# A first layer merged by a list scheduler: new weights, a longer lag, ranks for ties, and one affine folded into the MLP

## The chip, the cores and the metric

The kernel runs on one core of one Trainium2 chip. It computes two layers of a small vision network on 8 images of 64 x 64 pixels with 192 channels, all in float32. The metric is the device time of one execution in microseconds; before the change the median of three runs is 25196.08 us (25184.54 to 25197.58).

The core has five engines with a queue each, served in order: TensorE (PE: products and transposes; PEld is its weight load), VectorE (DVE), ScalarE (ACT: activations, from function tables that must be loaded), GpSimd (POOL), and SyncE (SP), which issues the transfers (DMA). An engine stalls when the head of its queue waits for another engine. So the order in which independent work is placed in the queues decides how long the engines stand idle.

## The reference

Each layer is `x = x + layer(groupnorm(x))`. Layer 0 is a block of two 3x3 depthwise convolutions, a state-space mixer and an MLP; layer 1 is a selective scan in four directions. The change is in layer 0, which is, cut to what matters:

```python
c1 = dwconv2d(x, cpe1_w, cpe1_b)                     # 3x3, per channel
xs = x + c1
h = layernorm(xs, ln1_w, ln1_b)                      # first norm
zxbcdt = h @ in_proj_w.T                             # z: 384, xBC: 512, dt: 6 columns
dt = softplus(dt + dt_bias)
xBC = silu(causal_conv1d(xBC, conv1d_w, conv1d_b))   # 4 taps
y = ssd(xm, dt, A, Bm, Cm, chunk)                    # chunked state-space mixer
y = (y + xm * D_skip) * silu(z)
y = y * rsqrt(mean(y * y) + 1e-05) * rms_w
x2 = xs + y @ out_proj_w.T
x2 = x2 + dwconv2d(x2, cpe2_w, cpe2_b)
h2 = layernorm(x2, ln2_w, ln2_b)                     # second norm: (x2 - mean) * rstd * w + b
m = gelu(h2 @ fc1_w.T + fc1_b) @ fc2_w.T + fc2_b
return x2 + m
```

## The kernel before

Layer 0 works on 64 tiles of 512 pixels (8 images of 8 tiles). Its work is written as 18 chains (Python generators), one for each stage, and each chain goes through all tiles. A chain yields steps: an engine, a weight (the time in us that the author expects of it), and the instructions. `Flow` merges the chains into one order for each engine, before anything runs, by a clock of its own: it always takes the step that can start first.

```python
class Flow:
    LAG, TABLE, STAY, RANK = 0.25, 1.3, 0.0, 0.01

    def chain(self, gen, rank=None, ready=0.0):
        self.chains.append([gen, next(gen), ready, len(self.chains) if rank is None else rank])

    def start(self, req, ready):
        # ... "wait" for another chain's mark, "take" of a buffer: come at once when possible
        engine, _, _, after, table = req
        t = max(ready if after is None else after, self.free[engine])
        if engine == "ACT" and table and table != self.table:
            return t + self.TABLE + self.STAY, t + self.TABLE
        return t, t

    def run(self):
        while self.chains:
            best = None
            for i, (_, req, ready, rank) in enumerate(self.chains):
                s = self.start(req, ready)
                if s and (best is None or s[0] + self.RANK * rank < best[0]):
                    best = s[0] + self.RANK * rank, s[1], i
            # ...
                engine, weight, do, _, table = req
                # ... the instructions are recorded, kept in this order on their engine
                t += weight
                self.free[engine] = t
                t += self.LAG          # from then on a dependent step may start
```

Layer 0 sets `f.RANK = -0.01`, so that with equal starts the chain that was entered later goes first; they are entered from the back of the network (MLP) to its front (statistics). The numbers of buffers are set there too and stay as they are:

```python
        f = Flow(tc)
        f.RANK = -0.01
        for tag, n in (("mm", 5), ("sm", 3), ("xin", 2), ("xs", 3), ("h", 3), ("cin", 2), ("cv", 2), ("zs", 2),
                       ("dt", 2), ("e", 5), ("yt", 4), ("yc", 1), ("xx", 3), ("x2", 1), ("m", 1), ("sq", 1), ("s2", 1), ("ld", 3), ("csr", 1), ("xdt", 1), ("xw", 1), ("t1", 1)):
            f.pool(tag, n)
```

`mm` and `sm` are PSUM banks, for wide and for small products. The stages that the text speaks of:

```python
        def conv(out, src, w, b):                # both 3x3 convolutions; line 325 is the tap
            for ct in range(CT):                 # CT = 2 halves of 96 channels
                r[ct] = yield step("ACT", 0.75, ...)      # first tap: scale and bias
            for j in range(1, 9):
                for ct in range(CT):
                    r[ct] = yield step("DVE", 0.75, lambda: [nc.vector.scalar_tensor_tensor(...)], r[ct])

        def norm(xs, w, b, key):
            # GpSimd adds the halves, PE takes the mean (ln_m), DVE subtracts, ACT squares,
            # GpSimd adds, PE takes the variance (ln_v), ACT: rs = exp(-0.5 * ln(var + eps))
            yield step("DVE", 1.25, lambda: [nc.vector.tensor_mul(h, h, bc(rs, 1, [CP, CT, TT]))])
            for ct in range(CT):                 # line 386: the affine
                r = yield step("ACT", 0.8, lambda: [
                    nc.scalar.activation(h[:, ct], h[:, ct], AF.Identity, bias=b[:, ct : ct + 1], scale=w[:, ct : ct + 1])])

        def rows_of(T, da):                      # running sums of the decays, for the e tiles
            # PE p_cs (line 598), ACT copies it to csr, SP writes csr to DRAM (csd)
        def decays():                            # SP reads csd back, spread over 128 rows, as e[T, c], 4 a tile
        def powers():
            # ACT: six Relu with a bias for each head (line 634), then one Exp (line 639), on e
        def scores():
            # PE p_g (line 654), DVE gm = p_g * mask, DVE e = e * gm (line 663)
        def turn():
            # PE p_t (transposes), DVE xdt and xw from it (lines 686, 691); PE p_b, ACT bt
        def states():
            # PE p_i, DVE t1; PE p_n, DVE st (the running state)
        def mixer():
            # PE p_y: three products with dsk (line 768), six with e and xdt (line 771);
            # DVE yt = t1 + p_y, yt = yt * zs
        def output():
            # ACT yt * rq, PE p_u (transposes), ACT yc, PE p_o, DVE xx = p_o + xs
        def mlp():
            # PE p_f (line 937, weights wf1 on h), ACT gelu (line 913, bias fb1), PE p_f (line 957), DVE, SP stores
```

At the end the chains are entered and merged:

```python
        for gen in (mlp, norm2, conv2, output, mixer, states, turn, scores, powers, decays, steps_in_time, convolve, mix, gate, norm1, conv1, inputs, statistics):
            f.chain(gen())
        f.run()
```

Layer 1 is drawn up by the same class with its standard figures in its short front and end parts, and by a fixed loop in its scan.

Of the kernel before, what the change touches and what calls it, by code (L numbers as in the profile page):

```python
# [16 lines left out]
CP, CT = 96, 2  # L17
# [168 lines left out]
def layer0(tc, consts, x, x1s, mv1, w_in, w_out, w_fc1, w_fc2, rows):  # L186
# [12 lines left out]
    with ExitStack() as ctx:  # L199
# [17 lines left out]
        nc.sync.dma_start(out=wf1, in_=w_fc1.rearrange("(t p) m -> p t m", p=CP))  # L217
        wf2 = wp.tile([128, 6, C], F32, name="wf2")
        nc.sync.dma_start(out=wf2, in_=w_fc2.rearrange("(t p) m -> p t m", p=128))
        rv = wp.tile([128, 12], F32, name="rv")  # L220
        nc.sync.dma_start(out=rv, in_=rows.partition_broadcast(128))
        dtb, an = rv[:, 0:6], rv[:, 6:12]
# [12 lines left out]
            nc.gpsimd.memset(t, 0.0)  # L235

        f = Flow(tc)
        f.RANK = -0.01
        for tag, n in (("mm", 5), ("sm", 3), ("xin", 2), ("xs", 3), ("h", 3), ("cin", 2), ("cv", 2), ("zs", 2),
                       ("dt", 2), ("e", 5), ("yt", 4), ("yc", 1), ("xx", 3), ("x2", 1), ("m", 1), ("sq", 1), ("s2", 1), ("ld", 3), ("csr", 1), ("xdt", 1), ("xw", 1), ("t1", 1)):  # L240
            f.pool(tag, n)
# [28 lines left out]
        def inputs():  # L270
            for T, (b, t) in enumerate(tiles):
                yield "wait", ("gn", b)
                yield "take", "xin"
                xin = got["xin", T] = xins[T % 2]
                lo, hi = max(0, t * RT - 1), min(HI, t * RT + RT + 1)
                at = lo - (t * RT - 1)

                def load():
                    out = []
                    for edge, row in ((t == 0, 0), (t == NT - 1, RT + 1)):  # L280
                        if edge:
                            f.keep(nc.gpsimd.memset(xin[:, :, row : row + 1, :], 0.0))
                    for ct in range(CT):
                        out.append(
                            nc.sync.dma_start(
                                out=xin[:, ct, at : at + hi - lo, 1 : WI + 1], in_=im(image(b)[:, ct, lo * WI : hi * WI])
                            )
                        )
                    return out

                r = yield step("SP", 0.2, load)
                sc, sh = got["gn", b]
                for ct in range(CT):
                    v = xin[:, ct, at : at + hi - lo, 1 : WI + 1]
                    r = yield step(
                        "ACT",
                        0.85,
                        lambda: [
                            nc.scalar.activation(v, v, AF.Identity, bias=sh[:, ct : ct + 1], scale=sc[:, ct : ct + 1])
                        ],  # L300
                        r + 4 if ct == 0 else None,
                    )
                f.at["in", T] = r

        def conv(out, src, w, b):

            tap = lambda ct, j: src[:, ct, j // 3 : j // 3 + RT, j % 3 : j % 3 + WI]
            r = [0.0] * CT
            for ct in range(CT):
                r[ct] = yield step(  # L310
                    "ACT",
                    0.75,
                    lambda: [
                        nc.scalar.activation(  # L314
                            im(out[:, ct]), tap(ct, 0), AF.Identity, bias=b[:, ct : ct + 1], scale=w[:, ct, 0:1]
                        )
                    ],
                )
            for j in range(1, 9):
                for ct in range(CT):  # L320
                    r[ct] = yield step(
                        "DVE",
                        0.75,
                        lambda: [
                            nc.vector.scalar_tensor_tensor(  # L325
                                im(out[:, ct]), tap(ct, j), w[:, ct, j : j + 1], im(out[:, ct]), ALU.mult, ALU.add
                            )
                        ],
                        r[ct],
                    )  # L330
            return max(r)
# [7 lines left out]
                f.give("xin", r)  # L339
                f.at["conv1", T] = r  # L340

        def norm(xs, w, b, key):

            yield "take", "h"
            h = got[key] = lnp.tile([CP, CT, TT], F32, name="h", bufs=3)
            both = lambda src: [nc.gpsimd.tensor_add(s2, src[:, 0], src[:, 1])]  # L346
            mean = lambda ps: [nc.tensor.matmul(ps[:CP], ones96, s2, start=True, stop=True)]
            yield "take", "s2"
            s2 = lnp.tile([CP, TT], F32, name="s2")
            yield step("POOL", 1.25, lambda: both(xs))  # L350
            yield "take", "mm"
            pm = mp.tile([128, TT], F32, name="ln_m", tag="mm")
            r = yield step("PE", 0.95, lambda: mean(pm))
            f.give("s2", r)
            r = yield step("DVE", 1.25, lambda: [nc.vector.tensor_sub(h, xs, bc(pm[:CP], 1, [CP, CT, TT]))])
            f.give("mm", r)
            yield "take", "sq"
            sq = lnp.tile([CP, CT, TT], F32, name="sq")
            yield step("ACT", 1.06, lambda: [nc.scalar.activation(sq, h, AF.Square)])  # L359
            yield "take", "s2"  # L360
            s2 = lnp.tile([CP, TT], F32, name="s2")
            r = yield step("POOL", 1.25, lambda: both(sq))
            f.give("sq", r)
            yield "take", "mm"
            pv = mp.tile([128, TT], F32, name="ln_v", tag="mm")
            r = yield step("PE", 0.95, lambda: mean(pv))
            f.give("s2", r)
            rs = lnp.tile([CP, TT], F32, name="rs", bufs=2)
            r = yield step(
                "ACT",  # L370
                1.3,
                lambda: [
                    nc.scalar.activation(rs, pv[:CP], AF.Ln, bias=eps[:CP]),
                    nc.scalar.activation(rs, rs, AF.Exp, scale=-0.5),
                ],
                None,
                "explog",
            )
            f.give("mm", r)
            yield step("DVE", 1.25, lambda: [nc.vector.tensor_mul(h, h, bc(rs, 1, [CP, CT, TT]))])  # L380
            for ct in range(CT):
                r = yield step(
                    "ACT",
                    0.8,
                    lambda: [
                        nc.scalar.activation(
                            h[:, ct], h[:, ct], AF.Identity, bias=b[:, ct : ct + 1], scale=w[:, ct : ct + 1]
                        )
                    ],
                )  # L390
            return r

        def norm1():
            for T in range(len(tiles)):
                yield "wait", ("conv1", T)
                f.at["h1", T] = yield from norm(got["xs", T], v96["l1w"], v96["l1b"], ("h1", T))

        def h1_done(T, r):
            if last := f.part(("h1", T), 2, r):
# [44 lines left out]
        def convolve():  # L444

            for T, (b, t) in enumerate(tiles):
# [9 lines left out]
                for pair in ((0, 1), (2, 3)):  # L456
                    for mt in pair:
                        yield "wait", ("cin", T, mt)
                        done[mt] = yield step(
                            "ACT",  # L460
                            0.68,
                            lambda: [
                                nc.scalar.activation(
                                    dst[mt],
# [7 lines left out]
                    for k in range(1, 4):  # L472
                        for mt in pair:
                            done[mt] = yield step(
                                "DVE",
                                0.9,
                                lambda: [
                                    nc.vector.scalar_tensor_tensor(
                                        dst[mt],
# [144 lines left out]
        def powers():  # L624

            for T in range(len(tiles)):
                for c in range(NQ):
# [1 line left out]
                    e, cs = got["e", T, c], got["cst", T]  # L629
                    yield step(  # L630
                        "ACT",
                        1.8,
                        lambda: [
                            nc.scalar.activation(e[:, h], e[:, h], AF.Relu, bias=cs[:, c, h : h + 1], scale=-1.0)
                            for h in range(NH)
# [6 lines left out]
        def scores():  # L642

            for T in range(len(tiles)):
                yield "wait", ("cv", T)
                bm, cm = got["bm", T], got["cm", T]
                for c in range(NQ):
# [12 lines left out]
                    yield "wait", ("p", T, c)  # L660
                    e = got["e", T, c]
                    f.at["e", T, c] = yield step(
                        "DVE", 0.95, lambda: [nc.vector.tensor_mul(e, e, bc(gm, 1, [128, NH, Q]))]
                    )

        def turn():
# [38 lines left out]
        def states():  # L705

            st = None
            for T, (b, t) in enumerate(tiles):
# [5 lines left out]
                for c in range(NQ):  # L714
# [23 lines left out]
                    else:  # L738
                        yield step(
                            "DVE",  # L740
                            0.55,
                            lambda: [nc.vector.tensor_mul(hv(new), hv(st), bc(dec[:NS, 2, c], 2, [NS, NH, HD]))],
                            0.0,
                        )
# [5 lines left out]
        def mixer():  # L750

            for T, (b, t) in enumerate(tiles):
# [3 lines left out]
                for c in range(NQ):  # L756
# [24 lines left out]
                    if t or c:  # L781
# [2 lines left out]
                        q = yield step("DVE", 0.55, lambda: [nc.vector.tensor_add(yt, t1, py)])  # L784
                        f.give("sm", q)
                        f.give("t1", q)
                        q = yield step("DVE", 0.62, lambda: [nc.vector.tensor_mul(yt, yt, zs[:, c])])
                    else:
                        q = yield step("DVE", 0.55, lambda: [nc.vector.tensor_mul(yt, py, zs[:, c])])
                        f.give("sm", q)  # L790
# [13 lines left out]
        def output():  # L804

            for T, (b, t) in enumerate(tiles):
# [14 lines left out]
                yc = tp.tile([128, 3, TT], F32, name="yc")  # L821
                for c in range(NQ):
                    yt = got.pop(("yt", T, c))
                    q = yield step("ACT", 0.52, lambda: [nc.scalar.activation(yt, yt, AF.Copy, scale=rs[:, c : c + 1])], r)
                    yield "take", "sm"
                    pt = qp.tile([128, DIN], F32, name="p_u", tag="sm")
                    q = yield step(
# [69 lines left out]
        def norm2():  # L897
            for T, (b, t) in enumerate(tiles):
# [2 lines left out]
                yield "take", "ld"  # L901
                xr = got["xr", T] = ld.tile([CP, CT, TT], F32, name="xr", tag="ld")
                yield step("SP", 0.1, lambda: [nc.sync.dma_start(out=xr, in_=image(b)[:, :, t * TT : t * TT + TT])])
                f.at["h2", T] = yield from norm(x2, v96["l2w"], v96["l2b"], ("h2", T))
                r = yield step("POOL", 2.7, lambda: [nc.gpsimd.tensor_add(xr, xr, x2)])
                f.give("x2", r)
                f.at["xr", T] = r
# [1 line left out]
        def keep_mlp(T, mt, m, ps, p):  # L909
            r = yield step(  # L910
                "ACT",
                0.69,
                lambda: [nc.scalar.activation(m[:, mt], ps, AF.Gelu, bias=v128["fb1"][:, mt : mt + 1])],  # L913
                p,
                "gelu",
            )
# [70 lines left out]
                if t == NT - 1:  # L987
                    yield step("DVE", 0.5, lambda: aggregate(nc, mv1[:, b], stats1))

        for gen in (mlp, norm2, conv2, output, mixer, states, turn, scores, powers, decays, steps_in_time, convolve, mix, gate, norm1, conv1, inputs, statistics):  # L990
            f.chain(gen())
        f.run()


# [825 lines left out]
```

## Time and profile before

| what | value |
|---|---|
| time, median of 3 | 25196.08 us |
| span of the profiled run | 25211.5 us |
| TensorE busy | 21347.4 us (85%) |
| VectorE busy | 21583.5 us (86%) |
| ScalarE busy | 21653.2 us (86%) |
| GpSimd busy | 16862.8 us (67%) |
| layer 0, from the timeline | 0 to about 5675 us |
| layer 1, the rest | about 19537 us |

The shares are means over two layers with different limits, so layer 0 has to be read from its own stretch. A stretch line gives the busy time of each engine in it, the number of instructions in brackets, and then the clock that TensorE was granted as a part of full speed. In a group's line, the first number after the bar is the busy time, the second the mean of one instruction in ns, and behind the next bar stands the idle time of the engine just before such instructions, with what ended it. The chain of waits is followed back from the last instruction: at each step to what released it.

### The profile page before, as it was taken

Reading aid. Unit: us, or ns where it says so; the run is one execution under the profiler, and the core shown is the slowest. Engines: PE = TensorE matmul, PEld = TensorE weight load, DVE = VectorE, ACT = ScalarE, POOL = GpSimd, SP = SyncE. Lnnn points to the kernel's source line nnn. Section 1 sums busy time; section 2 is a strip of 40 time slices with the busy share of each in tenths; the row PEclk is TensorE's granted clock in tenths of the full one; section 3 lists DMA queues with packets and bytes.
Section 4 is the critical chain, followed back from the end, with each engine's and each line's share of the span. In section 5 each row is a group of like instructions: output and inputs, shape, how many; then the busy total and the mean of one; then the engine's idle time right before and its main releaser. Section 6 shows DMA issues by size and latency. Waiting matters only on the chain.

```text
span 25211.5 us, 312991 instructions
## 1 busy us (share of the span) xinstructions
PE 21347.4 (85%) x100012; PEld 10381.6 (41%) x100012; DVE 21583.5 (86%) x22090; ACT 21653.2 (86%) x38251; POOL 16862.8 (67%) x13639
## 2 busy tenths in 40 slices
PE   7888888887888888888888888888888888888888
PEld 3444444443443444344434443444344434443444
DVE  6777667658999899899989998999899989988998
ACT  5666566558998999899989998999899989998998
POOL 0111111116997799599959995999599959986997
PEclk7888888888999999999999999999999999999999
DMA  1111111112222222222222222222222222222222
GB/s 45 38 36 42 37 37 42 33 28 88 66 66 76 78 65 69 85 68 65 66 88 66 66 66 87 66 66 69 85 67 67 64 89 65 67 66 87 66 66 59
DMA packets 1129703, 1608.06 MB, mean 64 GB/s; under 512 B 259360, under 2 KB 458432, under 8 KB 1118848
## 3 DMA queue, kind: packets, MB, share of 16 engines
q1 hardware_dynamic: 1128064, 1588.03, 22.4%
q8 instruction: 806, 13.21, 0.2%
q14 instruction: 833, 6.82, 0.1%
HBM read 1024.65 MB, written 160.17 MB: 47 GB/s over the span
## 4 chain that ended last, share of the span: by engine, by line
POOL 55%; PE 23%; issue 9%; DVE 6%; ACT 4%; DMA 3%; SPq 1%; POOLq 0%; DVEq 0%; ACTq 0%
POOL hc L1575 49%; POOL cy L1573 4%; DVE xs L1165 3%; PE p_f L937 2%; PE y L1590 2%; PE p_x L429 2%; PE p_f L957 2%; PE p_z L512 2%; POOL du L1454 1%; DMA xc<-xo 1%; PE p_y L771 1%; DVE xs L325 1%; PE p_o L854 1%; PE p_o L1339 1%; PE p_y L768 1%
## 5 line engine op out<-in xcount | busy, mean ns | idle before, releaser
L1575 POOL TENSOR_TENSOR hc<-hs,cb 128x1024 f32<-128x1024 f32 x6144 | 14582.9, 2374 | 10.4 <-POOL cy L1573 6.1
L1561 DVE TENSOR_TENSOR_SCAN hs<-ea,cy,g 128x512 f32<-128x512 f32 x10752 | 13058.6, 1263 | 787.6 <-PE g L1545 425.4
L1519 ACT ACTIVATE pw<-duT,bt 128x384 f32<-128x384 f32 x16384 | 8873.2, 601 | 12.8 <-DVE duT L1467 12.8
L1590 PE MATMUL y<-hc,sel 128*64 128x512 f32 x24576 | 6655.0, 620 | 2467.4 <-POOL hc L1575 2461.7
L1534 ACT ACTIVATE ea<-dr,an 128x512 f32<-128x512 f32 x12288 | 8125.5, 709 | 348.9 <-DVE hs L1561 326.2
L1545 PEld LDWEIGHTS g<-ident,pw 128*128 128x128 f32 x49152 | 5306.8, 141 | 4303.0 <-issue 2670.4
L1545 PE MATMUL g<-ident,pw 128*128 128x128 f32 x49152 | 6773.8, 280 | 30.6 <-DVE hs L1561 12.9
L1590 PEld LDWEIGHTS y<-hc,sel 128*64 128x64 f32 x24576 | 1228.9, 135 | 3886.9 <-POOL hc L1575 3627.0
L1573 POOL COPY cy<-hs 128x2 f32<-128x2 f32 x6144 | 1165.1, 190 | 1547.2 <-DVE hs L1561 1482.2
L1454 POOL TENSOR_TENSOR du<-de,xc 128x512 f32<-128x512 f32 x768 | 983.4, 1280 | 1639.2 <-DVE de L1447 1621.1
L1561 DVE TENSOR_TENSOR_SCAN hs<-ea,g 128x512 f32<-128x512 f32 x1536 | 1776.9, 1204 | 178.1 <-PE g L1545 122.7
L346 POOL TENSOR_TENSOR s<-x 96x512 f32<-96x512 f32 x64 | 88.5, 1383 | 2366.9 <-DVE x L325 2169.7
L346 POOL TENSOR_TENSOR s<-sq 96x512 f32<-96x512 f32 x128 | 221.2, 1728 | 1049.2 <-ACT sq L359 909.8
L1433 PE MATMUL p_dt<-xdbl,wd 13*128 13x512 f32 x1536 | 857.3, 639 | 41.4 <-DVE de L1447 39.5
L1165 DVE SCALAR_TENSOR_TENSOR xs<-pad,p,xs 128x4096 f32<-128x4096 f32 x192 | 860.8, 4484 | 36.9 <-ACT xs L1155 29.7
L1404 PE MATMUL p_d<-xc,wx 128*44 128x512 f32 x1536 | 792.1, 598 | 96.3 <-DMA xc<-xo 96.3
L937 PE MATMUL p_f<-h,wf 96*128 96x512 f32 x1536 | 786.4, 656 | 4.8 <-ACT m L913 3.3
L325 DVE SCALAR_TENSOR_TENSOR x<-xx,p,x 96x512 f32<-96x512 f32 x1024 | 720.2, 744 | 29.3 <-ACT x L314 29.1
L1447 DVE SCALAR_TENSOR_TENSOR de<-p_dt,spa 128x512 f32<-128x512 f32 x768 | 524.0, 682 | 255.6 <-ACT spa L1442 253.4
L325 DVE SCALAR_TENSOR_TENSOR xs<-xin,p,xs 96x512 f32<-96x512 f32 x1024 | 702.0, 755 | 17.2 <-ACT xs L314 17.2
L957 PE MATMUL p_f<-m,wf 128*96 128x512 f32 x1536 | 711.3, 614 | 0.8 <-ACT m L913 0.8
L1601 DVE TENSOR_TENSOR yacc<-yacc,y 128x512 f32<-128x512 f32 x576 | 624.6, 1084 | 18.5 <-PE y L1590 18.5
(199 smaller groups left out, 20330.1 us busy)
## 6 DMA issues: line engine op xcount, KB each, us to landing
cb<-cd SPq DMA_DIRECT2D x4096, 128.0 KB
dr<-de SPq DMA_DIRECT2D x3072, 128.0 KB
xc<-xo SPq DMA_DIRECT2D x256, 768.0 KB
e<-csd SPq DMA_DIRECT2D x256, 384.0 KB
xl<-x SPq DMA_DIRECT2D x256, 384.0 KB
xo<-xs SPq DMA_DIRECT2D x48, 1024.0 KB
xo<-xt SPq DMA_DIRECT2D x24, 2048.0 KB
xl<-in_x SPq DMA_DIRECT2D x64, 384.0 KB
```

The lines of the kernel that those rows point to most:

```text
L325: nc.vector.scalar_tensor_tensor(im(out[:, ct]), tap(ct, j), w[:, ct, j : j + 1], im(out[:, ct]), ALU.mult, ALU.add)
L937: nc.tensor.matmul(ps, wf1[:, ct, mt * 128 : mt * 128 + 128], h[:, ct], start=ct == 0, stop=ct == 1)
L957: nc.tensor.matmul(ps[:CP], wf2[:, kt, ct * CP : ct * CP + CP], m[:, kt], start=kt == 0, stop=kt == 5)
L1165: nc.vector.scalar_tensor_tensor(xs, tap(j), kw[:, d, j : j + 1], xs, ALU.mult, ALU.add)
L1454: o(nc.gpsimd.tensor_mul(st["du", d], st["de", d], st["xc"][:, d]))
L1519: nc.scalar.activation(st["pw", p, j][:, :, i], st["duT"][:, j].rearrange("p (g c) -> p g c", c=64), AF.Copy, scale=st["bt"][:, j, n : n + 1],
L1534: nc.scalar.activation(ea[:, f], state[s]["dr", d][:, f], AF.Exp, scale=an[:, k, p, at : at + 1])
L1545: nc.tensor.transpose(g[:, f, j * 128 : j * 128 + 128], state[s]["pw", p, j][:, 2 * d + f].rearrange("p a b -> p (a b)"), ident,)
L1561: nc.vector.tensor_tensor_scan(rev(h[:, f]), rev(ea[:, f]), rev(g[:, f]), 0.0 if first(s) else state[s - 1]["cy"][:, p, d, f : f + 1], ALU ...
L1573: o(nc.gpsimd.tensor_copy(st["cy"][:, p, d], h[:, :, last]))
L1575: o(nc.gpsimd.tensor_mul(hc, h, bc(st["cb", p], 1, [128, 2, TT])))
L1590: o(nc.tensor.matmul(y[half[f]], sel, hc[:, f], start=p == 0 and k > 0, stop=p == NP1 - 1))
```

## The change

The change draws the merged order of layer 0 anew and removes one small piece of its work.

- The weights of steps are set to what a profile measured, the lag after a step goes from 0.25 to 0.684 us, a switch of ScalarE's function table counts 0.464 us less in the choice of the next step (though not on the scheduler's clock), and each chain gets a rank of its own, which now decides ties only.
- The second norm's scale and shift (`ln2_w`, `ln2_b`) are applied to the first MLP product once, at the start: `wf1` is multiplied by the scale, and `fb1` becomes `fc1_b + fc1_w @ ln2_b`. The norm then ends with the multiplication by `rs`. The first norm keeps its affine.

```diff
+        ps = mp.tile([128, TT], F32, name="p_fb", tag="mm")
+        for mt in range(6):
+            for ct in range(CT):
+                nc.tensor.matmul(
+                    ps[:, mt : mt + 1],
+                    wf1[:, ct, mt * 128 : mt * 128 + 128],
+                    v96["l2b"][:, ct : ct + 1],
+                    start=ct == 0,
+                    stop=ct == 1,
+                )
+        fb1 = wp.tile([128, 6], F32, name="fb1")
+        nc.vector.tensor_add(fb1, ps[:, 0:6], v128["fb1"])
+        for ct in range(CT):
+            nc.vector.tensor_scalar_mul(wf1[:, ct], wf1[:, ct], v96["l2w"][:, ct : ct + 1])
 ...
-        f.RANK = -0.01
+        f.LAG, f.STAY, f.RANK = 0.684, -0.464, -0.01
 ...     # weights (engine, before -> after)
         # inputs' affine ACT 0.85 -> 0.92, first tap of conv ACT 0.75 -> 0.81
-        def norm(xs, w, b, key):
+        def norm(xs, key, w=None, b=None):
-            yield step("POOL", 1.25, lambda: both(xs))        # and both(sq)
+            yield step("POOL", 1.6, lambda: both(xs))
-            yield step("DVE", 1.25, lambda: [nc.vector.tensor_mul(h, h, bc(rs, 1, [CP, CT, TT]))])
-            for ct in range(CT):
+            r = yield step("DVE", 1.4, lambda: [nc.vector.tensor_mul(h, h, bc(rs, 1, [CP, CT, TT]))])
+            for ct in range(CT if w is not None else 0):
 ...     # causal convolution: first tap ACT 0.68 -> 0.81, further taps DVE 0.9 -> 0.77
         # powers: six Relu ACT 1.8 -> 2.35; scores: e * gm DVE 0.95 -> 1.02
         # states: st * dec DVE 0.55 -> 0.6; mixer: yt * zs DVE 0.62 -> 0.66; output: yt * rq ACT 0.52 -> 0.62
-                f.at["h2", T] = yield from norm(x2, v96["l2w"], v96["l2b"], ("h2", T))
+                f.at["h2", T] = yield from norm(x2, ("h2", T))
-                lambda: [nc.scalar.activation(m[:, mt], ps, AF.Gelu, bias=v128["fb1"][:, mt : mt + 1])],
+                lambda: [nc.scalar.activation(m[:, mt], ps, AF.Gelu, bias=fb1[:, mt : mt + 1])],
 ...
-        for gen in (mlp, norm2, conv2, output, mixer, states, turn, scores, powers, decays, steps_in_time, convolve, mix, gate, norm1, conv1, inputs, statistics):
-            f.chain(gen())
+        for gen, rank in (
+            (mlp, -0.177), (norm2, -0.056), (conv2, -0.275), (output, -0.03), (mixer, -0.08), (states, -0.04),
+            (turn, -0.06), (scores, 0.017), (powers, -0.284), (decays, -0.195), (steps_in_time, 0.209),
+            (convolve, 0.071), (mix, -0.12), (gate, -0.17), (norm1, -0.14), (conv1, -0.254),
+            (inputs, -0.313), (statistics, -0.298),
+        ):
+            f.chain(gen(), rank)
         f.run()
```

More of the change, by code (lines that the diff above doesn't have):

```diff
@@ L296, in inputs @@
                         "ACT",
-                        0.85,
+                        0.92,
                         lambda: [
@@ L311, in conv @@
                     "ACT",
-                    0.75,
+                    0.81,
                     lambda: [
@@ L361, in norm @@
             s2 = lnp.tile([CP, TT], F32, name="s2")
-            r = yield step("POOL", 1.25, lambda: both(sq))
+            r = yield step("POOL", 1.6, lambda: both(sq))
             f.give("sq", r)
@@ L395, in norm1 @@
                 yield "wait", ("conv1", T)
-                f.at["h1", T] = yield from norm(got["xs", T], v96["l1w"], v96["l1b"], ("h1", T))
+                f.at["h1", T] = yield from norm(got["xs", T], ("h1", T), v96["l1w"], v96["l1b"])
         def h1_done(T, r):
@@ L460, in convolve @@
                             "ACT",
-                            0.68,
+                            0.81,
                             lambda: [
@@ L475, in convolve @@
                                 "DVE",
-                                0.9,
+                                0.77,
                                 lambda: [
@@ L631, in powers @@
                         "ACT",
-                        1.8,
+                        2.35,
                         lambda: [
@@ L662, in scores @@
                     f.at["e", T, c] = yield step(
-                        "DVE", 0.95, lambda: [nc.vector.tensor_mul(e, e, bc(gm, 1, [128, NH, Q]))]
+                        "DVE", 1.02, lambda: [nc.vector.tensor_mul(e, e, bc(gm, 1, [128, NH, Q]))]
                     )
@@ L740, in states @@
                             "DVE",
-                            0.55,
+                            0.6,
                             lambda: [nc.vector.tensor_mul(hv(new), hv(st), bc(dec[:NS, 2, c], 2, [NS, NH, HD]))],
@@ L786, in mixer @@
                         f.give("t1", q)
-                        q = yield step("DVE", 0.62, lambda: [nc.vector.tensor_mul(yt, yt, zs[:, c])])
+                        q = yield step("DVE", 0.66, lambda: [nc.vector.tensor_mul(yt, yt, zs[:, c])])
                     else:
@@ L823, in output @@
                     yt = got.pop(("yt", T, c))
-                    q = yield step("ACT", 0.52, lambda: [nc.scalar.activation(yt, yt, AF.Copy, scale=rs[:, c : c + 1])], r)
+                    q = yield step("ACT", 0.62, lambda: [nc.scalar.activation(yt, yt, AF.Copy, scale=rs[:, c : c + 1])], r)
                     yield "take", "sm"
@@ L988, in mlp @@
                     yield step("DVE", 0.5, lambda: aggregate(nc, mv1[:, b], stats1))
-        for gen in (mlp, norm2, conv2, output, mixer, states, turn, scores, powers, decays, steps_in_time, convolve, mix, gate, norm1, conv1, inputs, statistics):
-            f.chain(gen())
+        for gen, rank in (
+            (mlp, -0.177),
+            (norm2, -0.056),
+            (conv2, -0.275),
+            (output, -0.03),
+            (mixer, -0.08),
+            (states, -0.04),
+            (turn, -0.06),
+            (scores, 0.017),
+            (powers, -0.284),
+            (decays, -0.195),
+            (steps_in_time, 0.209),
+            (convolve, 0.071),
+            (mix, -0.12),
+            (gate, -0.17),
+            (norm1, -0.14),
+            (conv1, -0.254),
+            (inputs, -0.313),
+            (statistics, -0.298),
+        ):
+            f.chain(gen(), rank)
         f.run()
```

## The prediction

> **What bounds the kernel now.** I read the page's span and slices first, then the busy time in stretches, then the chain of waits and the groups of layer 0. The slices show two programs: slices 1 to 9 with GpSimd almost idle (layer 0), the rest with GpSimd near full (layer 1). The timeline puts the last product of layer 0 at 5674 us, so layer 0 is 5675 us, 88.3 us for each of its 64 tiles (with 25 us of start taken off). Layer 1 is the other 19537 us, and the diff touches nothing in it.
>
> ```profile
> span 25211.5 us, 312991 instructions
> ...
> DVE  6777667658999899899989998999899989988998
> ACT  5666566558998999899989998999899989998998
> POOL 0111111116997799599959995999599959986997
> PEclk7888888888999999999999999999999999999999
> ```
>
> The stretch 600 to 5600 us is layer 0 in its steady state; two stretches of 90 us inside it are a bad and a good one (columns: length; busy time and instructions of PE, PEld, DVE, ACT and POOL in this order; granted TensorE clock, DMA share, GB/s).
>
> ```profile
> 600.00:5600.00 5000.00, 4375.39 (x13789) 2174.94 (x13789) 3480.66 (x5788) 3049.40 (x5662) 603.20 (x481) 0.85 0.14 37
> ```
>
> ```profile
> 2670.00:2760.00 90.00, 67.68 (x212) 34.75 (x212) 47.87 (x81) 33.79 (x68) 2.87 (x4) 0.74 0.10 23
> ```
>
> ```profile
> 2220.00:2310.00 90.00, 87.88 (x288) 41.50 (x287) 75.77 (x123) 66.38 (x114) 13.03 (x9) 1.00 0.17 45
> ```
>
> No engine is full. TensorE's 88% is time at a granted clock of 0.85. With full-clock durations (0.857 us for a 512-column product, 2.16 us for the nine of one y, and so on) the products of a tile add up to 60.3 us. VectorE is busy 70% of 88.3, or 61.5 us a tile, ScalarE 61%, or 53.9 us. So the floor of a tile is near 62 us, and 26 us are lost to waits in the merged order. The mean is 248 TensorE instructions in 90 us; the good stretch did 288, a tile in 88.3 x 248/288 = 76 us, with the clock at 1.00. The bad one did 212, a tile in 103 us.
>
> Why it is bad shows in the chain of waits there (start, length, what).
>
> ```profile
> 2652.25 0.98 PE p_cs L598 x8
> 2653.26 0.57 ACT csr L603
> 2653.86 1.51 DMA csd<-csr
> 2655.43 5.37 DMA e<-csd
> 2660.82 1.87 ACT e L634 x6
> ...
> 2698.02 1.30 PE p_y L771 x12
> 2699.34 5.54 DMA e<-csd
> 2704.95 1.87 ACT e L634 x6
> 2706.85 0.85 ACT e L639
> 2707.72 0.96 DVE e L663
> ...
> 2719.11 10.61 DVE xs L325 x16
> 2729.71 0.48 DVE xw L691
> 2730.24 0.27 PE p_b L696
> ```
>
> Two things to see: the decay tile e comes too late (product, copy, two transfers, seven activations, 14 us with nothing else on the chain), and sixteen taps of the first convolution stand as one block of 10.6 us on VectorE, with a 0.48 us operation behind them that TensorE wants.
>
> I added the whole chain over 600 to 5600 us by engine: PE 3475, DVE 605, ACT 516, DMA 167, POOL 82, issue 62 us. At 56.6 tiles that is 61.4 us a tile on TensorE (close to the 60.3 us at full clock) and 25.3 us off it. The 25.3 us are what an order can win.
>
> **What the skill says.** "TensorE: Matmul & The Clock Gate", Part 1: the array's clock is halved after a window of some 3.4 us without enough work. The trace fits: 1.00 in the fed stretch, 0.74 in the starved one; fewer holes should also raise the clock. "Perfetto Trace Analysis", Identifying the Most-Contended Engine: busy time of matmuls is no measure of the distance to the roof; here PE is 88% busy for about 68% worth of full-clock work, so I go by the chain. "ScalarE: Activation LUTs", What ACT_TABLE_LOAD costs: 1283 ns plus a drain near 1380 ns for a switch. The trace has the 1283 ns, but the idle time shown before loads is small, and at 5641 us the activation starts 1.29 us after its load does; I count 1.28 us.
>
> ```profile
> L169 ACT ACT_TABLE_LOAD x163 | 209.1, 1283 | 2.6
> ...
> L386 ACT ACTIVATE h<-h,p 96x512 f32<-96x512 f32 x252 | 196.3, 805 | 143.0 <-DVE h L380 142.8
> ```
>
> **The change, part by part.**
>
> *Second norm's affine moved into the MLP's weights.* It removes two of the L386 activations a tile, 128 in all: 128 x 0.805 = 103 us of ScalarE, or 1.6 us of its 53.9 a tile. ScalarE is not the bound, and the step lies between the norm and the MLP's products, where the order leaves room. It adds twelve one-column products, one addition and two scalings at the start, before the first statistics; VectorE waits there for its first input anyway until 14.1 us. I put 2 us on it.
>
> *Measured weights.* The scheduler's clock ran on guesses: the six Relu steps of e at 1.8 us (6 x 0.388 = 2.33 measured), the affine copies at 0.68 to 0.75 (0.80 measured), the causal taps at 0.9 (0.756 measured). The new figures are close to the groups. This makes no instruction shorter, it moves them.
>
> *Lag 0.25 to 0.684.* A real hand-over in the chain shows as 0.02 to 0.05 us of issue, so 0.684 is slack, not a measurement. It makes the order put other work between dependent steps.
>
> *Ranks.* Before, a tie went to the earlier stage of the network by up to 0.17 us, so with VectorE free and several things ready the convolution always won; that is how the blocks of 16 arise. Now ties differ by at most 0.005 us and the convolutions stand nearly last, as filler. I built the changed kernel and compared the listings of each engine's order: runs of 14 or more L325 taps fall from 68 to 5, and its blocks rise from 553 to 873. On TensorE I laid full-clock durations along the order: between p_cs and the first p_y of its tile, the tenth percentile of other work rises from 7.6 to 13.4 us (the e path takes about 12); between p_g and p_y from 6.1 to 10.4. The depth from p_x to the tile's last product falls from 409 to 348 us of work. Table loads fall from 471 to 424, the silu loads alone from 128 to 82: 47 x 1.28 = 60 us of ScalarE.
>
> *The sum.* From the chain over 56.6 tiles: the e path (csr 10, its two DMAs 24 and 139, ACT e 162 and 75, DVE gm and e 44) is 454 us; half should hide: 227. The xs taps are 243 us; with the blocks broken two thirds go: 160. The other 735 us (convolution two, the x, w and y multiplications, norms, copies) gain from slack, fewer loads and the dropped affine: I take a fifth, 147. Sum 534 us, 9.4 us a tile. Another wait comes last in part of these places, so I take off a tenth: 8.5 us a tile, a tile at 79.8 us, between the mean and the good stretch. Times 64, 544 us; less 2 us at the start, 542 us. 25196 - 542 = 24654, written as 24650, a ratio of 1.022.
>
> The halves and fifths are my choice; what is known is that 25.3 us a tile is the pot, and that the good stretch, made by luck, already gets 12 of them.
>
> **Rivals.**
> 1. *The order was never the limit, buffers are.* The buffer e has five slots, xdt and xw one each, the small PSUM tag three banks. VectorE waited 370 us for p_y ahead of xdt (138 times, the single slot), and the change leaves all counts alone. If these decide, the new order saves only the blocks and some loads, some 150 to 250 us: 24950 to 25050.
> 2. *The order comes near the floor.* Fewer holes keep TensorE's clock up, which shortens the products and leaves fewer holes. Were every stretch like the good one, a tile would be 76 us or less: 64 x 12.3 = 790 us, so 24400; at 74 us, 24280.
> 3. *The model's order is worse on the chip.* Starved convolutions leave later stages without work (the norms already wait 2107 us on GpSimd for x L325), and a shallower pipeline holds less in store. The listing speaks against it, as the short distances grew. It would be 25200 to 25500.
>
> **Range and chances.** I give my account about 0.55, rival 1 0.2, rival 2 0.2, rival 3 0.05. The time for 2% is 25196/1.02 = 24702, only 50 us above my number, so much of the middle lies on either side. Range 24340 to 24990. Faster 0.58, within 2% 0.40, slower 0.02.
>
> **What would show it.** Layer 0 should end near 5130 us and layer 1 last 19537 us within 20. In the steady stretch the clock should rise from 0.85 to about 0.9, VectorE's share from 70 to 77%, and ScalarE's total fall by some 160 us. In the chain, DMA e and DVE xs should be about half or less. Table loads should be 47 fewer. I am wrong if DVE xs leaves the chain and the tile still takes over 85 us (rival 1), if the tile goes below 76 (rival 2), or if layer 1 moves.

## The result and the profile after

The changed kernel takes 24392.6 us (median; 24386.46 to 24416.88) against 25192.64 us before: a ratio of 0.9685, 95% interval 0.9668 to 0.9701, or 800 us less. The page of its profiled run:

```profile
span 24390.1 us, 313055 instructions
...
DVE  7888888689988999899989998999899989998998
ACT  5666666589998999899889998998899899989998
POOL 1111111169976997799779977997799779977997
PEclk8999999989999999999999999999999999999999
```

GpSimd now fills up from the ninth slice, not the tenth, and TensorE's clock in the slices before stands at 9 tenths where it was at 8. In the timeline the last product of layer 0 ends at 4851 us instead of 5675. Layer 1 then lasts 24390 - 4851 = 19539 us, as before (19537). So all of the gain is in layer 0: a tile takes (4851 - 25)/64 = 75.4 us instead of 88.3. (The profiled run before was itself some 20 us above the median, so the two profiles are 821 us apart where the medians are 800.)

Two stretch lines of the changed kernel, the steady part of layer 0 and 90 us of it (length; busy time and instructions of PE, PEld, DVE, ACT, POOL; granted clock; DMA share; GB/s):

```profile
600.00:4800.00 4200.00, 3964.23 (x13614) 1957.90 (x13613) 3452.14 (x5693) 2820.35 (x5423) 601.62 (x473) 0.94 0.17 43
```

```profile
2600.00:2690.00 90.00, 88.90 (x316) 43.93 (x316) 76.77 (x127) 61.88 (x121) 14.97 (x8) 1.00 0.16 41
```

TensorE is busy 94.4% of the stretch (88% before) and its clock is 0.94 (0.85 before). VectorE is busy 82% (70%). What was a lucky stretch before, at 288 instructions in 90 us, is now below the usual: the mean is 13614/4200 x 90 = 292.

The chain of waits inside that stretch (start, length, what) shows what this is like:

```profile
2628.52 1.81 PE p_f L953 x4
2630.32 0.67 PE p_y L784 x6
2630.99 1.29 PE p_y L787 x12
2632.28 0.97 PE p_cs L614 x8
2633.25 0.20 PE p_b L712
2633.45 1.91 PE p_f L953 x4
...
2640.05 1.30 PE p_y L787 x12
2641.35 0.02 issue
2641.38 0.56 DVE xdt L702
2641.93 0.47 DVE st L761
2642.40 0.04 issue
2642.44 0.27 PE p_b L712
```

TensorE hands over to itself. After p_cs, which starts the e path (from that product to the finished tile e: the copy csr, its two transfers, the activations of e, and VectorE's gm and e), it goes on with other products, and the copy, the two transfers and the activations are nowhere on the chain in this stretch. What comes between is a short stay on VectorE. Added over the steady stretches, by tile (56.6 tiles before, 55.7 after; rounded):

| chain, us a tile | before | after |
|---|---|---|
| PE | 62.4 | 60.1 |
| DVE | 11.2 | 11.6 |
| ACT | 9.1 | 2.6 |
| DMA | 3.0 | 0.1 |
| POOL | 1.5 | 0.4 |
| issue | 1.1 | 0.7 |
| all | 88.3 | 75.4 |

What lies off TensorE fell from 25.9 to 15.3 us a tile.

The groups of layer 0 in the changed kernel show the same from the waiting side, and the dropped affine: ScalarE waited 27 us for the transfer of e before the Relu steps (145 us before the change, 134 of them for the transfer), and the affine is left for the first norm alone, 128 activations.

```profile
L650 ACT ACTIVATE e<-e,cst 128x128 f32<-128x128 f32 x1536 | 474.0, 389 | 27.3 <-DMA e<-csd 27.3
...
L402 ACT ACTIVATE h<-h,p 96x512 f32<-96x512 f32 x128 | 102.4, 805 | 46.0 <-DVE h L396 46.0
```

### The profile page after: what moved, and what is told of

It reads as the page before. It is cut to its first block, busy times and chain, and to the rows that moved or that the text cites. A ratio compares the mean times of both kernels' runs of the same rounds, so it can differ in the third digit from the quotient of the medians.

```text
span 24390.1 us, 313055 instructions
## 1 busy us (share of the span) xinstructions
PE 20962.6 (86%) x100036; PEld 10175.2 (42%) x100036; DVE 21614.8 (89%) x22093; ACT 21445.6 (88%) x38076; POOL 16900.2 (69%) x13639
## 4 chain that ended last, share of the span: by engine, by line
POOL 53%; PE 23%; issue 9%; DVE 7%; ACT 6%; DMA 1%; SPq 0%; POOLq 0%; DVEq 0%; ACTq 0%
POOL hc L1610 48%; POOL cy L1608 4%; PE p_f L953 3%; DVE xs L1200 2%; PE y L1625 2%; ACT pw L1554 2%; PE p_f L973 2%; ACT ea L1569 2%; PE p_x L445 2%; PE p_o L870 1%; POOL du L1489 1%; PE p_y L787 1%; PE p_z L528 1%; PE p_o L1374 1%; DMA xc<-xo 1%
## 5 line engine op out<-in xcount | busy, mean ns | idle before, releaser
L1580 PE MATMUL g<-ident,pw 128*128 128x128 f32 x49152 | 6771.8, 280 | 30.0 <-DVE hs L1596 12.9
L362 POOL TENSOR_TENSOR s<-xs 96x512 f32<-96x512 f32 x64 | 117.0, 1829 | 2035.0 <-DVE xs L340 1523.2
L340 DVE SCALAR_TENSOR_TENSOR x<-xx,p,x 96x512 f32<-96x512 f32 x1024 | 784.8, 814 | 15.3 <-ACT x L329 15.3
```

What stands on the lines that cost most here:

```text
L340: nc.vector.scalar_tensor_tensor(im(out[:, ct]), tap(ct, j), w[:, ct, j : j + 1], im(out[:, ct]), ALU.mult, ALU.add)
L1580: nc.tensor.transpose(g[:, f, j * 128 : j * 128 + 128], state[s]["pw", p, j][:, 2 * d + f].rearrange("p a b -> p (a b)"), ident,)
```

## The experiments

Labels that begin with b_ are the kernel before with one thing changed; those with a_ are the changed kernel with one thing changed. The runs were made in groups, each on another chip, and the time before was 25186 to 25204 us from one group to the next, so differences of 20 us between groups mean nothing. "Less" and "more" are against the kernel before in the same group for b_ runs, and against the 24392.6 us of the changed kernel for a_ runs.

### One part alone

**b_rank.** The new list of ranks, nothing else (so the sequence is new, and the ranks decide ties only):

```diff
-        for gen in (mlp, norm2, conv2, output, mixer, ...):
-            f.chain(gen())
+        for gen, rank in ((mlp, -0.177), (norm2, -0.056), ..., (statistics, -0.298)):
+            f.chain(gen(), rank)
```

> Kernel before with the new ranks alone (old weights, lag 0.25, table switch at its full cost, second norm's affine kept). Theory 1, ranks: the blocks of sixteen taps were the largest single loss, and ties between chains decide most of the order; the ranks alone should give 60 to 80% of the 800 us: 24550 to 24720 us, with DVE xs far down in the chain of waits. Theory 2, lag and weights: ties matter little while the scheduler's clock is wrong; the ranks give under 250 us: 24950 or more. Theory 3, removed work: under 150 us.

Measured: 24666.89 us, ratio 0.9793 (0.9778 to 0.9807), 519 us less. The time is the first theory's; its reason is not. The blocks are broken (7 runs of 14 or more taps are left of 68), and yet DVE xs is still 257 us of the chain, in smaller pieces, where it was 275. The e path is what shrank, from 456 to 110 us. The stretch line (600 us to the end of the steady part):

```profile
600.00:5081.00 4481.00, 4127.49 (x13527) 2047.53 (x13528) 3465.53 (x5682) 2815.37 (x5459) 640.72 (x473) 0.89 0.16 41
```

**b_lag.** `f.LAG, f.RANK = 0.684, -0.01`.

> Kernel before with the lag of 0.684 us alone. Theory 1, ranks: the lag helps the e path but the blocks of sixteen stay; 100 to 300 us: 24900 to 25100. Theory 2, lag and weights: over half of the 800 us: below 24790. Theory 3, removed work: within 100 us of before.

Measured: 25088.27 us, 0.9959 (0.9945 to 0.9974), 97 us less: just inside the first theory's range, and just inside the third's, which it therefore can't tell apart.

**b_weights.** The twelve weights of the diff.

> Kernel before with the measured weights alone. Theory 1, ranks: within 100 us of before, 25100 to 25290. Theory 2, lag and weights: 150 to 400 us faster, 24790 to 25040. Theory 3, removed work: within 50 us of before.

Measured: 25034.94 us, 0.9935 (0.9919 to 0.9952), 151 us less, more than the first theory said and at the upper edge of the second's range.

**b_fold.** The second norm's affine moved into `wf1` and `fb1`.

> Kernel before with the second norm's affine moved into the MLP's weights and nothing else (the order is drawn anew for the steps that are left). It takes 103 us of ScalarE away. Theories 1 and 2: ScalarE is not the bound, so 0 to 100 us, 25090 to 25190. Theory 3, removed work: ScalarE's chain is where the first layer waits, so 200 us or more: below 24990.

Measured: 25160.33 us, 0.9991 (0.9984 to 0.9998), 25 us less. A hundred microseconds of ScalarE taken out were worth a quarter of that; the third theory falls. At the start the product on the first statistics comes 2.1 us later (gn_ps at 30.62 instead of 28.52 us).

### Why the ranks

**b_conv.** The two convolutions are put last; the other ranks keep their sequence and their size of up to 0.17 us:

```diff
-            f.chain(gen())
+            f.chain(gen(), -1 if gen in (conv1, conv2) else i)   # i: its place in the list
```

> Kernel before with one difference: the two 3x3 convolutions come last in ties instead of second and third to last entered (all other ranks, weights and the lag as before). Theory A, filler: the ranks gained their 519 us because the convolutions stopped holding VectorE in blocks; this alone should bring 350 to 550 us, 24635 to 24835. Theory B, the whole set: the other ranks matter as much; under 250 us, 24935 or more.

Measured: 25247.16 us, 1.0020 (1.0009 to 1.0030), 56 us more. In the listing of its order only 3 runs of 14 or more taps are left of 68, and yet nothing is gained: theory B's side. The stretch line:

```profile
600.00:5669.00 5069.00, 4382.30 (x13725) 2187.91 (x13724) 3498.22 (x5742) 3003.55 (x5628) 624.23 (x475) 0.84 0.14 36
```

TensorE is busy 86.5% at a clock of 0.84, a little worse than before. The two convolutions did leave the chain in part, from 5.6 to 3.6 us a tile, but VectorE's other work on it rose from 5.6 to 8.4 us. So breaking the blocks is not what brought the gain. That the blocks cost nothing is not shown by it, since here a convolution also gives way to steps that start up to 0.18 us later.

**b_tie.** The old sequence of ranks, `f.RANK = -0.0001`.

> Kernel before with its old sequence of ranks, but a hundred times smaller, so that they decide ties only (as the new ranks do). Theory M, the size: the ranks gained because a later-stage step is no longer put off by up to 0.17 us for an earlier one; this alone should bring 300 us or more: below 24890. Theory S, the sequence: who wins the tie matters; within 150 us of before, 25040 to 25340.

Measured: 25112.08 us, 0.9964 (0.9951 to 0.9976), 92 us less: theory S. b_tie and b_rank both let ranks decide ties only, and differ in the sequence alone: 445 us between their medians, or 427 when each is taken against the kernel before of its own group.

**b_back.** `f.RANK = -0.0001` and `f.chain(gen(), -i)`: the back of the network wins.

> Kernel before with ranks for ties only and the sequence turned round: the back of the network (MLP) always wins, the statistics always lose. In the listing of orders it has the fewest table loads of all (322 against 471) but the shallowest pipeline (177 us of TensorE work from p_x to the tile's last product against 409). If fewer loads and finishing tiles early were what pays: below 24700. If a deep enough store of work between dependent steps is what pays: slower than before, 25300 to 26200.

Measured: 25582.65 us, 1.0153 (1.0138 to 1.0168), 378 us more. It has the fewest table loads (322) and is the slowest:

```profile
600.00:6013.00 5413.00, 4580.76 (x13759) 2261.44 (x13758) 3473.15 (x5756) 2838.74 (x5515) 567.59 (x475) 0.80 0.13 34
```

### One part left out

**a_rank.** The changed kernel with `f.chain(gen())` and the old list.

> Changed kernel with the old ranks (each chain's place, up to 0.17 us for the front of the network); weights, lag, cheaper table switch and the moved affine stay. If the parts add up (ranks 519 us of 793), 24392 + 519 = 24910 us, 24850 to 24980. If lag and weights are what the ranks need and also do most of it alone: below 24750.

Measured: 25065.89 us, 0.9952 (0.9938 to 0.9967), 673 us more than the changed kernel, above both expectations. The old list brings back the old sequence and also its size of up to 0.17 us, so the 673 us belong to both. Everything else without the ranks is worth 125 us.

**a_lag025.** `f.LAG = 0.25`.

> Changed kernel with the lag back at 0.25 us. If the parts add up (the lag alone gave 97 us): 24450 to 24540. If the lag pays only once ties no longer favour the convolutions: 24600 or more.

Measured: 24584.7 us, 0.9762 (0.9747 to 0.9776), 192 us more than the changed kernel, twice what the lag gave alone. It lies between the two expectations, at the edge of the second.

**a_nofold.** The second norm gets its affine back (`norm(x2, ("h2", T), v96["l2w"], v96["l2b"])`, the bias `v128["fb1"]`, no product at the start).

> Changed kernel with the second norm's affine back on ScalarE (128 activations of 0.8 us). If the parts add up (the move alone gave 25 us): 24390 to 24450. If ScalarE has become a limit in the tighter order: 103 us of work and more come back, 24490 or more.

Measured: 24333.76 us, 0.9661 (0.9646 to 0.9675): 59 us less than the changed kernel, although it has 103 us more to do on ScalarE. Neither expectation had this. It is the fastest version of the study, though its interval touches that of the changed kernel (0.9668 to 0.9701).

```profile
600.00:4740.00 4140.00, 3925.82 (x13569) 1939.39 (x13569) 3430.22 (x5680) 2869.93 (x5515) 619.64 (x473) 0.95 0.17 44
```

### How rough, and buffers

**a_lag070.** `f.LAG = 0.70`.

> Changed kernel with the lag at 0.700 instead of 0.684 us, a change that means nothing in itself; it shows how rough the landscape of orders is. If the gain lies in the kind of order: 24392 within 60 us. If 0.684 was found by trying and fits by luck: 80 to 250 us slower, 24470 to 24640.

Measured: 24374.38 us, 0.9673 (0.9659 to 0.9688), 18 us less. So the gain is no luck of this one figure.

**a_xdt2.** `xdt` has two buffers in the pool and in the scheduler's count, `gm` one.

> Changed kernel with two xdt buffers instead of one (gm gets one instead of two, to make room), so that VectorE need not wait for the y products before it writes the next xdt: 285 us of idle VectorE stand before xdt in the changed kernel. If buffers are the limit that is left: 100 us or more faster, below 24290. If VectorE's wait there costs nothing because TensorE sets the pace: within 60 us, 24330 to 24450.

Measured: 24366.72 us, 0.9671 (0.9656 to 0.9685), 26 us less. VectorE's wait ahead of xdt in the steady stretch (who waited for whom; us in total, times, longest), in the changed kernel:

```profile
DVE xdt L702 <- PE p_y L787: 284.9, 120, 8.7
```

and with two buffers:

```profile
DVE xdt L702 <- PE p_y L787: 58.5, 31, 5.1
```

226 us of idle time went and the end moved by 26. Part of it came back at the next single buffer, xw, for which VectorE now waits 78 us; in all, its idle time in the steady stretch fell from 748 to 676 us. This buffer is not the limit. (gm lost a buffer in the same run, so the price of that is in it too.) Two buffers for xw as well, and more PSUM banks for the small products, were not tried.

### All runs side by side

Steady part of layer 0 (55 to 57 tiles): TensorE's busy share and clock from the stretch lines, and the e path in the chain of waits, added up.

| run | us | PE busy | clock | e path, us |
|---|---|---|---|---|
| b_back | 25583 | 84.6% | 0.80 | 303 |
| b_conv | 25247 | 86.5% | 0.84 | 319 |
| before | 25193 | 87.5% | 0.85 | 456 |
| b_fold | 25160 | 87.5% | 0.86 | 346 |
| b_tie | 25112 | 88.3% | 0.84 | 382 |
| b_lag | 25088 | 88.0% | 0.86 | 214 |
| a_rank | 25066 | 88.0% | 0.86 | 222 |
| b_weights | 25035 | 88.6% | 0.87 | 225 |
| b_rank | 24667 | 92.1% | 0.89 | 110 |
| a_lag025 | 24585 | 93.5% | 0.90 | 62 |
| changed | 24393 | 94.4% | 0.94 | 60 |
| a_lag070 | 24374 | 94.1% | 0.95 | 106 |
| a_xdt2 | 24367 | 94.1% | 0.95 | 93 |
| a_nofold | 24334 | 94.8% | 0.95 | 90 |

The time goes with TensorE's share and clock, and with the e path only roughly: b_lag takes 242 us of it off the chain and gains 97. When one wait is hidden, another comes last in part of the places. The share is no cause by itself: the products are the same in all runs, so any wait that goes raises it. Nor was the clock changed alone.

## Why the prediction was right, point by point

It said 24650 with a range of 24340 to 24990 and faster by over 2% as the likeliest; 24392.6 lies in the range, near its fast end, and the gain is 800 us where 542 were expected. It was right that the order loses the time in layer 0 and that the new one wins part of it back. It came out a third too low, and one of its own signs of being wrong came true: the tile went below 76 us, to 75.4. By that sign its second rival is what happened (every stretch like the good one; a chance of 0.2, and 24400 us).

- **What bounds the kernel.** Right that the order is what loses time and that layer 1 is untouched: layer 1 moved by 2 us, and the gain lies in layer 0 alone. The floor of 62 us a tile is not tested, as the fastest version of the study stands at 74.5.
- **The reading of the chain.** Its sums leave out 93 us of the 5000. Added without gaps, TensorE has 3532 us (not 3475), VectorE 637 (not 605), and the xs taps in it 275 (not 243). What lies off TensorE is then 25.9 us a tile, not 25.3, which changes little.
- **The affine.** Right that ScalarE is no bound and that the start costs some 2 us. Its worth is within the roughness of the order: 25 us alone, and its return in a_nofold even gained.
- **Table loads.** 47 fewer, as the listing had it, but b_back shows that they do not decide: 149 fewer than before and slower.
- **The lag.** Right in kind: it is slack and not a measured delay, and 0.70 serves as well as 0.684. b_lag and a_lag025 put it at 97 to 192 us.
- **The ranks.** Right that they matter, wrong in why. The prediction named the blocks of sixteen taps; b_conv broke them and gained nothing, and in the changed kernel the convolutions' two terms in the chain (xs and x) went from 5.6 to 5.4 us a tile. The xs term alone fell nearly as said (275 to 132 us, where 160 us were to go), but what it gave up came back at the second convolution (x, 42 to 166 us).
- **The e path.** "Half should hide" was too low: 456 to 60 us of the chain, 7.0 us a tile instead of 4.0.
- **The rest.** 12.3 to 8.9 us a tile, 3.4 where a fifth was put at 2.6.
- **The reading of short distances in the order.** Weak. The tenth percentiles that were held to speak for the change (13.4 us after p_cs, 10.4 after p_g) are about 13 and 10 in the order of b_fold, which gained 25 us.
- **The sum.** The terms off TensorE came to 9.4 us a tile and were 10.6 in the end (7.0 for e, 0.2 for the convolutions, 3.4 for the rest), so that they came close is luck: errors of 3.0 and 0.8 us one way (e and the rest) met one of 2.6 us the other (the convolutions). The tenth taken off for new waits, 9.4 to 8.5, was not needed. And there was no term for TensorE itself, whose pieces of the chain fell by 2.3 us a tile; 10.6 + 2.3 = 12.9 us, the whole difference of 88.3 and 75.4.
- **The clock.** Named in the second rival and left out of the sum. TensorE's busy time in the steady part, for the same products, fell from 77.2 to 71.2 us a tile (a ratio of 0.92), while the clock rose from 0.85 to 0.94 (0.85/0.94 = 0.90). So the products got shorter about as the clock went up. How much of the 2.3 us on the chain that makes is not shown: b_rank has only 58.2 us of TensorE a tile there, at a clock of 0.89.
- **The other signs.** Layer 0 was to end near 5130 us (4851), the clock to reach about 0.9 (0.94), VectorE's share 77% (82%), ScalarE's total to fall by 160 us (208), DMA e and DVE xs to half or less (139 to 0 us, and 275 to 132). All went the way that was said, most of them further; the table loads alone came as listed.
- **The first rival, buffers.** Refuted by the result itself, as all counts of buffers stayed and 800 us went where it allowed 250; with a second buffer for xdt the end moved by another 26 us alone.

What stays open: which of the ranks does it, and why this sequence hides the e path. The sequence as a whole is shown to be worth about 430 us on the kernel before (b_tie against b_rank); in the changed kernel, sequence and size together are worth 673 us (a_rank). Back first, the old sequence, and the old sequence with the convolutions last come nowhere near it; no other sequence was tried, so nothing says how rare a good one is. The cheaper table switch in the choice of steps was not tried by itself, and the weights were not left out of the changed kernel. The four parts alone sum to 519 + 97 + 151 + 25 = 792 us, close to the whole, but left out one at a time three of them are worth 673, 192 and -59, so the sum is a coincidence and not a proof of independence.

## What to carry to other kernels

When no engine is full and an order drawn up in advance feeds them, the pot is the part of the chain that lies off the busiest engine. It is an estimate of the most that hiding waits can win, of which the changed kernel got a part: 10.6 of 25.9 us a tile. Add the chain up until it covers the whole stretch, and look at the busiest engine's own time as well, which may fall too (77.2 to 71.2 us a tile here, with the clock at 0.94 instead of 0.85). A striking block in the chain is a symptom until an order without it has been timed: breaking it moved the time to other work on the same engine. In a greedy merge the sequence of priorities among chains can outweigh the weights and the lag, and a small change of work (25 us one way, 59 the other here) disappears in the roughness of the order.

## What the runs showed of the hardware

Taps on VectorE that ran beside an addition on GpSimd often took much longer, with no dependence between the two. In the changed kernel's timeline (start, length), GpSimd adds a 96x1024 tile while VectorE's tap, 0.74 us as a rule, takes 2.84 us:

```profile
2599.26 2.67 POOL L921 TENSOR_TENSOR xr<-xr,x 96x1024 f32<-96x1024 f32 x1
```

```profile
2599.64 2.84 DVE L340 SCALAR_TENSOR_TENSOR xs<-xin,p,xs 96x512 f32<-96x512 f32 x1
```

Of the 2048 taps of layer 0 in the changed kernel, 107 took over 1 us, and every one of them overlapped an addition on GpSimd; the 1778 that overlapped none took 0.78 us at most. Another 163 overlapped one and stayed short. Before the change 23 taps were that long. With the tighter order the mean of the second convolution's taps rose from 744 to 814 ns, though their median stayed at 737 to 739 ns. That the GpSimd addition causes the long taps is read from these overlaps and was not tried by itself.
